# A two-layer vision tower: the late pieces of layer 1's feed-forward on earlier half-steps

## The chip, the cores and the metric

The kernel runs on one core of a Trainium2 chip. The metric is the device time of one execution in microseconds; before the change the median of three runs is 2030.3 us (2027.38 to 2031.56). All data are 32-bit floats.

## The reference

32 images of 256x256 pixels are cut into 256 tokens of width 256, and go through two layers of attention and feed-forward. The change touches the last part alone, the feed-forward of layer 1, a mixture of attention experts in four heads of width 64. Cut to what matters (n is the head, e the expert, d the width of a head):

```python
sx = einsum('bsh,ndh->bnsd', x, hl_w) + hl_b                  # head layer
q, k, v = ...                                                 # four experts' queries per head, one key, one value
att = softmax(einsum('bnesd,bntd->bnest', q, k) * d ** 0.5 + causal)
out = einsum('bnest,bntd->bnesd', att, v)
gs = softmax(einsum('bnsf,nef->bnse', out, gate_w) + gate_b)
mixed = einsum('bnsed,bnse->bnsd', out, gs)                   # experts mixed by their gates
hn = layernorm(mixed + resid)
hx = relu(fx @ fc1_w.T + fc1_b)                               # fx is hn; first layer
hx = layernorm(hx @ fc2_w.T + fc2_b + fx)                     # second layer, late norm
fg = softmax(fout @ fgate_w.T)                                # fout is hx, over the four heads
return fout * fg[..., None]                                   # added to h by the caller
```

## The kernel before

The stage works on an image in pieces, and each piece has a half-step at which it runs, counted from the image's own start. Images start six half-steps apart, so several are in flight, and the pieces of different images are interleaved. The order of instructions is fixed by the program: each engine works through its own instructions in the order in which this loop writes them, and an instruction that isn't ready holds up all that follow it on that engine.

```python
SCORES, VALUES, LAST = 6, 11, 46
EARLY = ((32, post, 9), (22, post, 15))
PIECES = (
    (0, prep, 0), (42, post, 12), (30, post, 16), (18, post, 1),
    (25, post, 5), (7, prep, 7), (31, post, 8), (19, post, 2),
    (26, post, 6), (44, post, 13), (2, prep, 2),
    (45, post, 14), (33, post, 10), (21, post, 3),
    (28, post, 7), (40, post, 11),
    (23, post, 4), (17, post, 0), (-1, prep, -1),
)

def pieces(t, table):
    for step, do, i in table:
        b, r = divmod(t - step, 6)
        if r == 0 and 0 <= b < B:
            do(b, images[b], i)

for t in range(-1, 6 * (B - 1) + LAST):
    active = [(images[b], t - 6 * b) for b in range(B)]
    if t % 2 == 0:
        ...                                  # scores of two parts, expert products (A), head values
        pieces(t, EARLY)
        ...                                  # masks and exponentials of the scores, copies of the products
    pieces(t, PIECES)
    ...                                      # values: exponentials times head values, at half-steps 11, 13, 15
```

An even half-step and the odd one after it make a round; the six half-steps from one image's start to the next are rounds one, two and three. In each round TensorE has scores (products of 64 rows, two at a time in the two halves of the rows), in rounds one and three expert products in the same form, and values (products of 64 columns, two at a time). A "full product" takes all 128 rows and all 128 columns.

The masks and exponentials (`weights`), with L1038 and L1040 of the profile:

```python
nc.vector.tensor_tensor(own, own, over(tri, [P, n_e, P], 1), ALU.add)     # L1038, in the scores' bank
t = pt.tile([P, 512], F32, name="et")
nc.scalar.activation(t, p, AF.Exp)                                        # L1040
```

The pieces that the change moves, and those on which they depend (cuts marked by dots):

```python
if i == 2:   ...                             # gates; both mixing products on GpSimd (L1118)
if i == 3:   ...                             # VectorE: sums of the mix, to im.r ("er")
if i == 15:  im.sq = squares(im.r)           # ScalarE
if i in (4, 10):
    nc.vector.tensor_reduce(ss, im.sq, AX.X, ALU.add)                     # L1131
    im.rs = head_rstd(ss)                                                 # GpSimd, L1069 and L1070 ("hv")
    if i == 10 and b % 8 == 7:
        check_ranges(b)                                                   # two VectorE instructions
if i == 5:
    nc.vector.tensor_tensor(im.r, im.r, over(im.rs, G8, 2), ALU.mult)     # L1136, er
if i == 6:
    p = feature_major(im.r...)                                            # four transposes of er
    nc.scalar.activation(im.fT..., p, AF.Identity, bias=col("e_b"), scale=col("e_g"))   # fxT
if i == 7:
    mm(p, fc1, im.fT...)                                                  # the first layer, a full product
    nc.scalar.activation(im.hx..., p, AF.Relu, bias=col("fc1_b"))
    ...                                                                   # four DMAs: both <- fxT, hx
if i == 8:   ...                             # second layer (W,both), VectorE copies to ey
if i == 9:   im.sq = squares(im.y[:, :, 0:HD])
if i == 11:  ...                             # VectorE: enorm <- ey * rs; head gate, its exponential
if i == 12:  ...                             # four transposes of enorm; ScalarE to foT
if i == 13:  ...                             # four transposes of foT (L1192)
if i == 14:  ...                             # VectorE: fout <- transposed * gate, + h; DMA to the output
```

All of TensorE's results go through eight PSUM banks of 512 columns, handed out in turn. `fxT`, `hx`, `both`, `enorm`, `foT` and `fout` have one buffer each, `ey` has two.

Of the kernel before, what the change touches and what calls it, by code (L numbers as in the profile page):

```python
# [79 lines left out]
def vit_tower(tc, a, out):  # L80
# [847 lines left out]
    with (  # L928
# [166 lines left out]
        def post(b, im, i):  # L1095
# [113 lines left out]


        images = [Image() for _ in range(B)]
        SCORES, VALUES, LAST = 6, 11, 46
        EARLY = ((32, post, 9), (22, post, 15))
        PIECES = (
            (0, prep, 0), (42, post, 12), (30, post, 16), (18, post, 1),
            (25, post, 5), (7, prep, 7), (31, post, 8), (19, post, 2),
            (26, post, 6), (44, post, 13), (2, prep, 2),
            (45, post, 14), (33, post, 10), (21, post, 3),
            (28, post, 7), (40, post, 11),
            (23, post, 4), (17, post, 0), (-1, prep, -1),  # L1220
        )

# [424 lines left out]
```

## Time and profile before

| What | us | share of the span |
| --- | --- | --- |
| span of the profiled run | 2025.9 | |
| TensorE busy | 1953.6 | 96% |
| VectorE busy | 1316.5 | 65% |
| ScalarE busy | 823.9 | 41% |
| GpSimd busy | 726.8 | 36% |
| layer 1's feed-forward, from the first mask to the end | 707.2 | 35% |
| of it, after the last mask | 67.8 | 3% |

In the profile PE is TensorE, PEld its loading of weights, DVE VectorE, ACT ScalarE and POOL GpSimd. A line of the order of time has the start of a group of like instructions, its length in us, the engine, the line of the program, the operation, what it writes and reads, and in brackets how long the engine sat idle before it and which instruction ended that. All matrix products have the line of one helper, L115, and are told apart by their tiles. The ends of matrix products are modelled, so starts are the safer times. Each product of 32-bit floats leaves two records.

### The profile page before, as it was taken

The numbers are of one execution on the slowest core, as the hardware profiler recorded it, in microseconds if no ns is written. First come the engines' busy times: TensorE is split into PE (matmuls) and PEld (weight loads), VectorE is DVE, ScalarE is ACT, GpSimd is POOL, SyncE is SP. The second block draws the span as 40 slices with busy tenths as digits, with TensorE's granted clock in tenths as the row PEclk, the third lists the DMA queues.
The fourth block names the chain that finished last, engine by engine and source line by source line (L and its number), as shares of the span: only waits on it lengthen the run. The fifth ranks groups of instructions, "written<-read, shape, count | busy, mean of one in ns | idle before, by whom it ended". The sixth has DMA issues, their size and how long they took to land.

```text
span 2025.9 us, 37649 instructions
## 1 busy us (share of the span) xinstructions
PE 1953.6 (96%) x15108; PEld 1374.2 (68%) x15108; DVE 1316.5 (65%) x3605; ACT 823.9 (41%) x1549; POOL 726.8 (36%) x692
## 2 busy tenths in 40 slices
PE   9998999999999989999899999999999999999984
PEld 8885676766666757666455555577777777777762
DVE  2335557676665653443556465567889999998986
ACT  0001312122222112212444444377777777777761
POOL 1224215243432342434333433203444443434443
PEclk9999999999999999999899999999999999999996
DMA  9440000000000141221000000001212121221211
GB/s 301 150 139 1 0 0 32 16 27 11 22 13 19 36 147 50 78 68 58 11 0 1 1 1 0 0 23 33 54 49 59 49 59 49 54 54 46 62 49 54
DMA packets 69813, 95.09 MB, mean 47 GB/s; under 512 B 8576, under 2 KB 51200, under 8 KB 69248
## 3 DMA queue, kind: packets, MB, share of 16 engines
q1 hardware_dynamic: 62912, 75.04, 13.0%
q0 software_dynamic: 6144, 16.79, 2.7%
q8 instruction: 121, 1.98, 0.4%
q10 hardware_dynamic: 576, 0.79, 0.1%
q14 instruction: 60, 0.49, 0.1%
HBM read 46.45 MB, written 20.97 MB: 33 GB/s over the span
## 4 chain that ended last, share of the span: by engine, by line
PE 94%; DVE 3%; ACT 1%; DMA 1%; POOL 0%; issue 0%; SPq 0%; ACTq 0%; DVEq 0%
PE bank L115 88%; PE bank L688 2%; PE bank L188 1%; PE bank L1192 1%; PE bank L350 0%; DMA both<-hx 0%; ACT bxT L193 0%; PE bank L241 0%; DVE fout L1201 0%; DMA tokW<-in_tokW_dram 0%; DVE bx L174 0%; DVE ctmp L357 0%; DVE fout L1197 0%; DVE two L1123 0%; DVE ctmp L355 0%
## 5 line engine op out<-in xcount | busy, mean ns | idle before, releaser
L1040 ACT ACTIVATE et<-bank 128x512 f32<-128x512 f32 x384 | 202.3, 598 | 58.5 <-DVE bank L1038 57.9
L115 PEld LDWEIGHTS bank<-ev,et 128*64 128x64 f32 x6144 | 198.4, 137 | 33.3 <-ACT et L1040 20.6
L115 PE MATMUL bank<-ev,et 128*64 128x74 f32 (+1 forms) x6144 | 211.3, 227 | 0.0
L1038 DVE TENSOR_TENSOR bank<-bank,w_tri 128x256 f32<-128x256 f32 (+1 forms) x384 | 173.6, 515 | 55.6 <-PE bank L115 53.7
L1118 POOL TENSOR_TENSOR eo<-eo,gate 128x1024 f32<-128x1024 f32 x64 | 121.9, 1925 | 215.7 <-DVE gate L1115 203.1
L115 PE MATMUL bank<-g,sx 64*128 64x512 f32 (+1 forms) x512 | 191.0, 502 | 1.4 <-ACT g L998 1.4
L115 PE MATMUL bank<-g,sw 64*128 64x512 f32 (+1 forms) x512 | 189.6, 502 | 0.0
L115 PE MATMUL bank<-tokW,patch 128*128 128x256 f32 x768 | 168.0, 382 | 0.3 <-DMA tokW<-in_tokW_dram 0.3
L115 PEld LDWEIGHTS bank<-tokW,patch 128*128 128x128 f32 x768 | 146.8, 191 | 21.6 <-DMA tokW<-in_tokW_dram 1.3
L115 PE MATMUL bank<-bxT,w_wuv 128*128 128x512 f32 x320 | 147.9, 601 | 6.6 <-ACT bxT L193 4.0
L193 ACT COPY bxT<-bank 128x512 f32<-128x512 f32 x16 | 9.4, 586 | 341.4 <-PE bank L188 341.4
L1070 POOL TENSOR_TENSOR hv<-hv,minus_half 128x8 f32<-128x8 f32 x64 | 119.6, 1868 | 5.3
L1056 ACT COPY eo<-bank 128x286 f32<-128x286 f32 x256 | 97.3, 421 | 58.5 <-PE bank L115 52.0
L115 PE MATMUL bank<-wvo,dm 128*128 128x512 f32 x256 | 114.0, 598 | 0.0
L115 PE MATMUL bank<-xsel,w_w 128*128 128x512 f32 x256 | 113.4, 601 | 0.0
L115 PE MATMUL bank<-attn,bv 128*128 128x256 f32 x512 | 113.3, 379 | 0.0
L115 PE MATMUL bank<-w_wo,gT 128*128 128x256 f32 x512 | 113.1, 379 | 0.0
L115 PE MATMUL bank<-w_w,hT 128*128 128x256 f32 x512 | 113.1, 379 | 0.0
L115 PE MATMUL bank<-w_wuv,bxT 128*128 128x512 f32 x256 | 112.5, 592 | 0.0
L115 PEld LDWEIGHTS bank<-attn,bv 128*128 128x128 f32 x512 | 97.1, 190 | 19.5 <-issue 6.7
L115 PEld LDWEIGHTS bank<-w_w,hT 128*128 128x128 f32 x512 | 96.7, 190 | 15.8 <-issue 3.4
L1069 POOL TENSOR_SCALAR hv<-ranges 128x8 f32<-128x8 f32 x64 | 39.1, 610 | 189.8 <-DVE ranges L1131 189.6
(258 smaller groups left out, 3861.8 us busy)
## 6 DMA issues: line engine op xcount, KB each, us to landing
patch<-in_patches_dram SPq DMA_DIRECT2D x31, 768.0 KB, 4.8
sw<-sx SPq DMA_DIRECT2D x64, 128.0 KB, 2.4
both<-fxT SPq DMA_DIRECT2D x64, 128.0 KB, 2.4
both<-hx SPq DMA_DIRECT2D x64, 128.0 KB, 2.3
out_dram<-fout SPq DMA_DIRECT2D x32, 256.0 KB, 2.4
cs<-ranked SPq DMA_DIRECT2D x32, 128.0 KB, 3.8
results<-cy SPq DMA_DIRECT2D x32, 128.0 KB, 1.7
w_w<-in_w_dram SPq DMA_DIRECT2D x2, 1024.0 KB, 6.1
```

What stands on the lines that cost most here:

```text
L115: nc.tensor.matmul(o, lhsT, rhs, start=first, stop=last)
L188: nc.tensor.transpose(p[:, o : o + P], x[:, c, k * P : (k + 1) * P], ident)
L193: nc.scalar.copy(o, i)
L688: nc.tensor.transpose(p[:, o : o + P], x[:, c, k * P : (k + 1) * P], ident)
L1038: nc.vector.tensor_tensor(own, own, over(tri, [P, n_e, P], 1), ALU.add)
L1040: nc.scalar.activation(t, p, AF.Exp)
L1056: nc.scalar.copy(im.o[:, c * NH + n, 0:OC], p[:, 0:OC])
L1069: nc.gpsimd.tensor_scalar(v, x, 1.0 / HD, 1e-8, ALU.mult, ALU.add)
L1070: nc.gpsimd.tensor_tensor(v, v, minus_half, ALU.pow)
L1118: nc.gpsimd.tensor_tensor(im.mix[k], im.mix[k], over(im.gate[:, :, 2 * k : 2 * k + 2], [P, NC * NH, 2, HD], 3), ALU.mult)
L1192: nc.tensor.transpose(im.po[:, o : o + P], im.fT[:, k, c * P : (c + 1) * P], ident)
```

## The change

Two things move, and nothing is added or removed. The last four pieces of an image (11 to 14: late norm, its transposes, the transposes back, the output) run six half-steps sooner, in the same places of a round, so that the loop is six half-steps shorter. The transposes of `er` (piece 6) move from the start of the second round to the end of the first, just behind the piece that makes `er`; and the first layer (piece 7) moves from the third round to the second. What it is for: with fc1 gone, the third round holds no full product among its products of half rows and half columns, and the schedule has a shorter tail.

```diff
-        SCORES, VALUES, LAST = 6, 11, 46
+        SCORES, VALUES, LAST = 6, 11, 40
         EARLY = ((32, post, 9), (22, post, 15))
         PIECES = (
-            (0, prep, 0), (42, post, 12), (30, post, 16), (18, post, 1),
-            (25, post, 5), (7, prep, 7), (31, post, 8), (19, post, 2),
-            (26, post, 6), (44, post, 13), (2, prep, 2),
-            (45, post, 14), (33, post, 10), (21, post, 3),
-            (28, post, 7), (40, post, 11),
+            (0, prep, 0), (36, post, 12), (30, post, 16), (18, post, 1),
+            (25, post, 5), (25, post, 6), (7, prep, 7), (31, post, 8), (19, post, 2),
+            (38, post, 13), (2, prep, 2), (26, post, 7),
+            (39, post, 14), (33, post, 10), (21, post, 3),
+            (34, post, 11),
             (23, post, 4), (17, post, 0), (-1, prep, -1),
         )
```

Within a round the order of VectorE's instructions stays as it was. TensorE's order changes: round one ends with the transposes of `enorm`, then those of `er`, then the second layer and the values; round two has scores, transposes of `foT`, head layer, first layer, values; round three has scores, expert products, values.

## The prediction

> **What bounds the kernel now.** I read the busy shares first, then the busy time by stage, then the order of time of single engines in one image of layer 1's feed-forward. Everything before that stage is untouched: the change moves pieces of this schedule alone.
>
> ```profile
> PE 1953.6 (96%) x15108; PEld 1374.2 (68%) x15108; DVE 1316.5 (65%) x3605; ACT 823.9 (41%) x1549; POOL 726.8 (36%) x692
> ```
>
> TensorE is busy almost throughout; but a share of the whole says nothing of one stage. The busy times of two stretches, 32 images in full swing and the run-out (columns: span, then busy us of each engine):
>
> ```profile
> 1431.63:1904.90 473.27, 473.27 (x7240) 369.03 (x7240) 429.25 (x1181) 358.87 (x783) 202.00 (x138) 1.00 0.21 53
> 1958.00:2025.90 67.90, 31.29 (x338) 23.23 (x332) 47.99 (x131) 18.54 (x39) 24.28 (x18) 0.69 0.19 52
> ```
>
> In full swing TensorE is busy 473.27 of 473.27 us, and the list of waits has no TensorE wait in that stretch; VectorE is busy 429.25, or 91%. So VectorE has little air. The run-out, 68 us, is a chain of latencies with TensorE less than half busy. Now one image, by TensorE's order of time (start, duration, in us):
>
> ```profile
> 1637.35 1.17 PE L115 MATMUL bank<-W,both 128*64 128x68 f32 x32
> 1638.35 2.16 PE L115 MATMUL bank<-ev,et 128*64 128x74 f32 x64
> ...
> 1642.36 0.66 PE L688 MATMUL bank<-ident,er 128*128 128x128 f32 x4
> 1642.86 0.60 PE L1192 MATMUL bank<-ident,foT 128*128 128x128 f32 x4
> 1643.29 1.89 PE L115 MATMUL bank<-exT,w_hl 128*128 128x256 f32 x8
> 1645.12 2.21 PE L115 MATMUL bank<-ev,et 128*64 128x74 f32 x64
> ...
> 1650.04 1.12 PE L115 MATMUL bank<-fxT,w_fc 128*128 128x512 f32 x2
> 1651.09 2.21 PE L115 MATMUL bank<-ev,et 128*64 128x74 f32 x64
> ...
> 1657.36 0.60 PE L688 MATMUL bank<-ident,enorm 128*128 128x128 f32 x4
> 1657.89 1.17 PE L115 MATMUL bank<-W,both 128*64 128x68 f32 x32
> ```
>
> The second layer (W,both) recurs after 1657.89 - 1637.35 = 20.54 us: the period of an image. The same image on VectorE:
>
> ```profile
> 1636.54 0.68 DVE L1136 TENSOR_TENSOR er<-er,hv 128x512 f32<-128x512 f32 x1
> ...
> 1641.60 1.96 DVE L1038 TENSOR_TENSOR bank<-bank,w_tri 128x512 f32<-128x512 f32 x4 [1.46 <-PE bank L115]
> ...
> 1648.73 1.95 DVE L1038 TENSOR_TENSOR bank<-bank,w_tri 128x256 f32<-128x256 f32 x4
> ...
> 1654.39 1.62 DVE L1038 TENSOR_TENSOR bank<-bank,w_tri 128x256 f32<-128x256 f32 x4
> ...
> 1657.08 0.69 DVE L1136 TENSOR_TENSOR er<-er,hv 128x512 f32<-128x512 f32 x1
> ```
>
> VectorE waits for TensorE once, 1.46 us before the second round's masks (L1038), and is then dense until L1136 has scaled `er`. That ends at 1637.22; TensorE passes from `enorm` to W,both at 1637.35. Only 0.13 us lie between them, and exactly there the change puts the transposes that read `er`. This is the line to watch.
>
> **What the Trainium skill says.** TensorEngine Tiling (Array Packing), Key Properties: changing the tiling mode drains TensorE. The trace agrees: the four expert products (sx,A, row halves) take 1655.92 - 1655.05 = 0.87 us before another product in row halves, but 0.96 before the full fc1; and fc1 takes 1.05 from its start to the next, where half of the 1.71 of w_hl (1.83 less some 0.12 for its own change of mode) is 0.86. SBUF — State Buffer, on the two separate sides: VectorE and GpSimd share a port pair, and the later of them blocks. The trace agrees: L1083 takes 0.26 at 1643.86 and ends with the gate products on GpSimd (1640.29 + 3.81 = 1644.10). Perfetto Trace Analysis, Tensor Engine Instruction: matmul ends are estimated. So I count from start to start.
>
> **The change part by part**, for one image. A round is two half-steps; rounds one, two and three make six.
>
> TensorE alone. The third round loses fc1: 0.96 + 1.05 = 2.01 become 0.87 plus one direct change from row to column halves, which no run shows yet; estimate 0.10, so 0.97. The second round gains fc1 behind other full products: 0.86. The four `er` transposes (0.5) move from round two to the end of round one, beside other transposes: nothing. Sum: 20.54 - 2.01 + 0.97 + 0.86 = 20.36, a gain of 0.18. No instruction disappears.
>
> The new wait. The `er` transposes now stand straight after L1136 and ahead of W,both. Follow the loop from the end of L1136 at 0. VectorE to TensorE takes 0.06 (in the run-out `enorm` ends at 2014.58 + 0.69 and its transposes start at 2015.33). Transposes to W,both 0.53 (1657.36 to 1657.89), W,both 1.00, values 2.09: the second round's scores start at 3.68, where they start at 1640.44 - 1637.22 = 3.22 now. Scores 1.92, foT 0.43, then w_hl and fc1 1.71 + 0.86 + 0.12 = 2.69, values 2.13: the third round's scores start at 10.85, against 1647.25 - 1637.22 = 10.03 now.
>
> The third of that round's four masks needs the last score. The first round shows how long that takes: its masks end at 1656.01, the last two take 0.33 + 0.42, so the third starts at 1655.26, 2.03 after the scores began at 1653.23 (and the 1.62 there, where four such masks take 4 x 0.33 + 0.1, shows the wait). In the third round the mask now starts at 1648.73 + 0.66 = 1649.39, or 12.17, and the last score would allow 12.06: 0.11 of slack. After the change it can't start before 10.85 + 2.03 = 12.88, 0.71 later. From there to the end of L1136 VectorE is dense. Without its small wait in round one that loop lasts 20.29 (L1136 at 1595.68 and 1615.97, while VectorE caught up), so 20.29 + 0.71 = **21.00 us per image**, 0.46 over 20.54. TensorE, able to do 20.36, would wait about 0.64 for `er` in every image.
>
> The sum over the stage. L1136 of the images ends at 1372.9 (image 0), 1925.2 (27), 1945.3 (28). The first periods, with little late work, gain less: +0.2 and +0.9, then +1.3 as the four late pieces join an image earlier. The 24 periods from image 3 to 27 last 1925.19 - 1431.63 = 493.6 now and 24 x 21.00 = 504.0 then: +10.4. Image 27 to 28: +0.2. In every eighth image the range check adds two instructions of some 0.6 us to VectorE. Today they are absorbed by its air (the periods then run 21.5 and 20.3, 20.3, ... with TensorE unmoved); in the new loop about 0.85 of 1.2 remains, three times: +2.5. Together +15.5.
>
> The run-out. Six half-steps less do not mean an image's work less: all pieces remain, and only the chain of image 31 counts. Its gain: `enorm` of image 31 now waits at 2014.58 behind the output of image 30, although its factor left GpSimd at 2010.75; fewer foreign pieces lie ahead of its end. I work this out as -2. Its loss: W,both now waits behind transposes that wait for `er`; near 1979 that shifts the second layer from 1978.3 to about 1980, near 1964 by some 1.4, and the late norm, now one half-step behind its GpSimd factor (about 2.6 us), waits 0.9 more. Together about +4; net +2. The total is 15.5 + 2 = +17.5, or 2048; because rival A pulls one way only, I put 2046.
>
> **Rivals.** A: TensorE stays the bound and keeps its 0.18 in all images, and the run-out shrinks by 2 to 6: 2030.3 - 5.8 - 4 = 2020. For it speaks that TensorE has no wait today and that 0.13 us are a positive slack; against it, that `er` itself hangs on TensorE's scores, so that the slack is consumed as soon as the transposes push them back. B: the new wait comes, but only the second round's masks hold VectorE back (4.84 against 4.38, of which L1083 hides 0.09): 20.29 + 0.37 = 20.66 per image, with the range checks at full length 24 x 0.12 + 3.6, and with the start and run-out about +9: 2039. C: the shorter tail is worth a whole image of the run-out, 10 to 15 us, and pays for everything: about 2030. Against it, that the last images are bound by VectorE, GpSimd and DMA in turn, whose work is all still there.
>
> **Range and chances.** The loop's sum has seven terms, each good to some 0.03; 0.2 per image either way are 5 us, the run-out is good to 6, and A or B might hold in part. So 2046 with 2033 to 2058. Two per cent are 40.6 us: slower by that much would need 1.4 us per image, faster has no mechanism. Faster 0.01, same 0.96, slower 0.03.
>
> **What would show it.** Right: a list of waits in full swing in which TensorE's transposes wait for VectorE's L1136, 0.3 to 0.7 us in each image; a period near 21.0; a small wait of L1038 for TensorE in round three, and about 1.8 in place of 1.46 in round two; experts straight into values within 1.0 us. Wrong: a period under 20.5 without that wait (A), one of 20.65 without a wait in round three (B), or a stage that ends more than 5 us earlier after image 31's `er` (C). The prediction would be wrong above all if VectorE's chain shortens where GpSimd's port no longer blocks it, or if the change of mode costs far more than 0.1.

## The result and the profile after

The change makes the kernel slower: 2054.4 us (median of four runs, 2053.7 to 2055.4) against 2029.9; the ratio is 1.0122, with a 95% interval of 1.0105 to 1.0140. The prediction said 2046 and 2033 to 2058.

First the busy times by stage, in the columns of the prediction (span, then busy us of PE, PEld, DVE, ACT and POOL): full swing from image 3's to image 27's L1136, then the run-out from the last mask.

```profile
1436.56:1948.17 511.61, 493.11 (x7536) 386.42 (x7536) 446.20 (x1231) 384.03 (x817) 210.93 (x144) 1.00 0.21 51
1982.00:2053.10 71.10, 27.78 (x322) 21.39 (x318) 45.15 (x120) 17.55 (x36) 23.91 (x18) 0.65 0.16 42
```

The same 24 images take 511.6 us where they took 493.6, and TensorE, which was busy for all of 493.6 us there, now idles for 18.5 us of 511.6. The list of waits for TensorE in full swing (1432 to 1925 us), which was empty before, has two rows (waiting engine and line, what released it, us in total, times, longest):

```profile
PE bank L688 <- DVE er L1136: 16.5, 23, 0.8
PE bank L115 <- ACT g L998: 1.3, 3, 0.4
```

There are 23 waits of 0.7 us, one in each image, for the instruction that scales `er`; the three of the second row fall in the three periods with a range check. Where the wait for `er` sits in TensorE's order of time, for one image:

```profile
1648.38 0.60 PE L688 MATMUL bank<-ident,enorm 128*128 128x128 f32 x4
1649.68 0.63 PE L688 MATMUL bank<-ident,er 128*128 128x128 f32 x4 [0.70 <-DVE er L1136]
1650.24 1.17 PE L115 MATMUL bank<-W,both 128*64 128x68 f32 x32
...
1655.25 0.66 PE L1192 MATMUL bank<-ident,foT 128*128 128x128 f32 x4
1655.74 1.89 PE L115 MATMUL bank<-exT,w_hl 128*128 128x256 f32 x8
1657.47 1.02 PE L115 MATMUL bank<-fxT,w_fc 128*128 128x512 f32 x2
1658.42 2.21 PE L115 MATMUL bank<-ev,et 128*64 128x74 f32 x64
...
1660.56 0.69 PE L115 MATMUL bank<-g,sw 64*128 64x512 f32 x1
...
1662.39 1.03 PE L115 MATMUL bank<-sx,A 64*128 64x256 f32 x8
1663.35 2.21 PE L115 MATMUL bank<-ev,et 128*64 128x74 f32 x64
...
1670.91 0.63 PE L688 MATMUL bank<-ident,er 128*128 128x128 f32 x4 [0.70 <-DVE er L1136]
```

What the change was for is there too: fc1 costs 0.95 beside other full products (1657.47 to 1658.42) where it cost 1.05, and the expert products go straight into values after 0.96 (1662.39 to 1663.35). But from one image's transposes of `er` to the next it is 21.23 us (1649.68 to 1670.91). VectorE in the same image:

```profile
1648.85 0.68 DVE L1136 TENSOR_TENSOR er<-er,hv 128x512 f32<-128x512 f32 x1
...
1654.49 1.96 DVE L1038 TENSOR_TENSOR bank<-bank,w_tri 128x512 f32<-128x512 f32 x4 [1.81 <-PE bank L115]
...
1661.72 0.76 DVE L1038 TENSOR_TENSOR bank<-bank,w_tri 128x256 f32<-128x256 f32 x2
1662.65 1.30 DVE L1038 TENSOR_TENSOR bank<-bank,w_tri 128x512 f32<-128x512 f32 x2 [0.17 <-PE bank L115]
...
1670.08 0.68 DVE L1136 TENSOR_TENSOR er<-er,hv 128x512 f32<-128x512 f32 x1
```

The wait in round two has grown from 1.46 to 1.81, and in round three, where the four masks were one dense group, the group is now split by a wait of 0.17 for the last score. VectorE waits for TensorE's scores, and TensorE waits for VectorE's `er`, once around in each image: neither is full, and the loop is the bound.

### The profile page after: what moved, and what is told of

It is laid out like the page before. It is cut to its first block, busy times and chain, and to the rows that moved or that the text cites. A ratio compares the mean times of both kernels' runs of the same rounds, so it can differ in the third digit from the quotient of the medians.

```text
span 2053.1 us, 37650 instructions
## 1 busy us (share of the span) xinstructions
PE 1952.3 (95%) x15108; PEld 1376.4 (67%) x15108; DVE 1313.7 (64%) x3605; ACT 834.9 (41%) x1549; POOL 726.1 (35%) x692
## 4 chain that ended last, share of the span: by engine, by line
PE 81%; DVE 15%; issue 1%; POOL 1%; ACT 1%; DMA 0%; SPq 0%; DVEq 0%; ACTq 0%
PE bank L115 77%; DVE bank L1038 4%; PE bank L688 1%; DVE ranges L1131 1%; PE bank L188 1%; DVE enorm L1172 1%; DVE er L1136 1%; DVE junk L982 1%; PE bank L1192 1%; DVE ex L174 1%; DVE sm_m L1075 1%; PE bank L350 0%; POOL hv L1070 0%; DVE lg L1104 0%; ACT bxT L193 0%
## 5 line engine op out<-in xcount | busy, mean ns | idle before, releaser
L1040 ACT ACTIVATE et<-bank 128x512 f32<-128x512 f32 x384 | 207.3, 599 | 75.8 <-DVE bank L1038 73.3
```

## The experiments

Theory: the loss is the loop `er` (VectorE) - its transposes, second layer, values, scores (TensorE) - masks (VectorE) - `er`. Rivals: the late pieces, now just behind their GpSimd factor, hold VectorE up; or the new order of TensorE's products (and with it the turns of the PSUM banks) costs in itself. Seven kernels, each compared with the kernel before on the same chip. The period is that of an undisturbed image; "24 images" is from image 3's L1136 to image 27's; "run-out" from image 28's L1136 to the end; all three are from the profiled run.

| kernel | median us | ratio to before (95%) | period | 24 images | run-out |
| --- | --- | --- | --- | --- | --- |
| before | 2028 to 2030 | | 20.53 | 493.6 | 80.6 |
| the change | 2054.4 | 1.0122 (1.0105 to 1.0140) | 21.23 | 511.6 | 84.3 |
| late pieces only | 2027.1 | 0.9991 (0.9984 to 0.9998) | 20.53 | 493.3 | 77.3 |
| `er` transposes and first layer only | 2054.0 | 1.0120 (1.0103 to 1.0137) | 21.23 | 511.7 | 86.3 |
| first layer back in round three | 2043.7 | 1.0065 (1.0048 to 1.0082) | 20.75 | 501.7 | 85.0 |
| `er` scaled earlier | 2030.3 | 1.0008 (0.9999 to 1.0017) | 20.34 | 491.1 | 85.3 |
| `er` transposes in round two | 2022.4 | 0.9974 (0.9967 to 0.9980) | 20.34 | 491.1 | 75.7 |
| `er` transposes behind W,both | 2031.0 | 1.0012 (1.0005 to 1.0019) | 20.64 | 497.4 | 76.6 |
| as the last but one, first layer in round three | 2027.3 | 0.9986 (0.9977 to 0.9994) | 20.53 | 493.3 | 77.7 |

**The late pieces only.** The kernel before, with

```diff
-        SCORES, VALUES, LAST = 6, 11, 46
+        SCORES, VALUES, LAST = 6, 11, 40
-  (42, post, 12)  (44, post, 13)  (45, post, 14)  (40, post, 11)
+  (36, post, 12)  (38, post, 13)  (39, post, 14)  (34, post, 11)
```

> Only the four late pieces run six half-steps sooner; the transposes of er and the first layer stay where they were. Theory (the loss is the new loop er - transposes - scores - masks - er, and the late pieces have no part in it): the period of an image stays 20.5 us, the run-out gets 2 to 4 us shorter, about 2027. Rival (the late pieces, now one half-step behind their GpSimd factor, hold VectorE up and cost the period): period near 21.2 and about 2050.

Measured: 2027.1, period 20.53, run-out 3.2 shorter. The late pieces cost no period: that rival falls.

**The transposes of er and the first layer only.** The change, with the late pieces back on 40, 42, 44, 45 and LAST 46.

> Only the transposes of er and the first layer move; the late pieces stay on their old half-steps. Theory (new loop): period 21.2 us as in the whole change, TensorE waits about 0.7 us for L1136 in each image, and without the gain of the late pieces in the run-out about 2057. Rival (late pieces): period near 20.4, about 2026.

Measured: 2054.0, period 21.23. The whole loss is in this half. I had expected 3 us more: beside this half the late pieces gain only 2.0 in the run-out (86.3 to 84.3), and they cost 1.2 in the first images (image 0's L1136 to image 3's lasts 60.15 here and 61.31 in the change).

**The first layer back in round three.**

```diff
-            (38, post, 13), (2, prep, 2), (26, post, 7),
+            (38, post, 13), (2, prep, 2),
-            (34, post, 11),
+            (28, post, 7), (34, post, 11),
```

> As the whole change, but the first layer goes back to the third round; only the er transposes stay behind L1136. Theory (two gates in series: the second round's masks, and, because fc1 stands ahead of it, the third round's masks): the wait of L1038 in the third round disappears, the second round's remains near 1.8 us, and the period falls from 21.23 to about 20.8; about 2043. If the transposes alone made the whole loss, the period stays at 21.2 and the time at 2054; if fc1's place made it, the period is 20.5 and the time about 2032.

Measured: 2043.7, period 20.75. VectorE's order of time for one image of this kernel:

```profile
1664.46 0.68 DVE L1136 TENSOR_TENSOR er<-er,hv 128x512 f32<-128x512 f32 x1
1670.10 1.96 DVE L1038 TENSOR_TENSOR bank<-bank,w_tri 128x512 f32<-128x512 f32 x4 [1.81 <-PE bank L115]
1677.12 1.95 DVE L1038 TENSOR_TENSOR bank<-bank,w_tri 128x256 f32<-128x256 f32 x4
1682.73 1.41 DVE L1038 TENSOR_TENSOR bank<-bank,w_tri 128x256 f32<-128x256 f32 x4
1685.21 0.68 DVE L1136 TENSOR_TENSOR er<-er,hv 128x512 f32<-128x512 f32 x1
```

Round two's wait stays at 1.81, and round three's masks are dense again (1.95 in one group). TensorE still waits for `er`, but so briefly that no bracket marks it; the starts show it:

```profile
1685.41 0.60 PE L688 MATMUL bank<-ident,enorm 128*128 128x128 f32 x4
1686.04 0.63 PE L688 MATMUL bank<-ident,er 128*128 128x128 f32 x4
```

From `enorm` to `er` it is 0.63, where the next kernel, with `er` there in time, has 0.44; and 1686.04 is 0.15 after the end of L1136 (1685.21 + 0.68 = 1685.89). So the 0.70 us of the period are two gates in series: 0.22 from the transposes of `er` (20.75 - 20.53), and 0.48 from fc1 standing ahead of round three's scores (21.23 - 20.75).

**er scaled earlier on VectorE.**

```diff
-            (0, prep, 0), (36, post, 12), (30, post, 16), (18, post, 1),
-            (25, post, 5), (25, post, 6), (7, prep, 7), (31, post, 8), (19, post, 2),
+            (0, prep, 0), (36, post, 12), (24, post, 5), (30, post, 16), (18, post, 1),
+            (25, post, 6), (7, prep, 7), (31, post, 8), (19, post, 2),
```

> As the whole change, but VectorE scales er (L1136) ahead of the zero count and of the gate's row in the same round, some 1.15 us sooner; no TensorE instruction moves. Theory (TensorE waits for L1136): the loop becomes 21.23 - 1.15 = 20.1 us, TensorE is the bound again at 21.23 - 0.84 = 20.4, the wait for L1136 is gone except after range checks; about 2032 (the run-out stays some 4 us longer than before). Rival (the order of TensorE's products, changes of mode and weight loads make the loss): the period stays at 21.2 and the time at 2054.

Measured: 2030.3, period 20.34, with the order of TensorE's instructions, and the turns of the banks with it, as in the change. TensorE's order of time has the three groups without a gap:

```profile
1676.42 0.60 PE L688 MATMUL bank<-ident,enorm 128*128 128x128 f32 x4
1676.86 0.60 PE L688 MATMUL bank<-ident,er 128*128 128x128 f32 x4
1677.39 1.17 PE L115 MATMUL bank<-W,both 128*64 128x68 f32 x32
```

The second rival falls: the order of products is no loss, but a gain of 0.19 once `er` is there in time. Yet the total does not beat the kernel before: the run-out, counted from an L1136 that stands earlier in its round here, is still 85 us.

**The transposes of er behind the second layer.**

```diff
-  (25, post, 5), (25, post, 6), (7, prep, 7), (31, post, 8), (19, post, 2),
+  (25, post, 5), (7, prep, 7), (31, post, 8), (25, post, 6), (19, post, 2),
```

> As the whole change, but within the first round the transposes of er stand behind the second layer (W,both) in place of ahead of it. Theory: the second layer's 1.00 us falls out of the loop, 21.23 - 1.00 = 20.2, so TensorE is the bound at 20.34 and up to 0.2 for two more changes of mode, 20.5; in the run-out the second layer no longer waits for er, so that the last image's chain gets back the 4 to 5 us which the change and the early er both lost there; about 2027. If the run-out's loss has another cause (the late norm half a round behind its factor), the run-out stays at some 84 us after image 28's er and the time is about 2034.

Measured: 2031.0, period 20.64, run-out 76.6. Right on the run-out, too low by 4 us on the time: four transposes between products of column halves cost 0.30 an image more than beside other transposes, where I allowed 0.2 (the period is 20.64, and 20.34 with `er` scaled earlier; TensorE has no wait for `er` in either). In the run-out TensorE's order of time of the change has, for images 30 and 31,

```profile
2005.74 1.09 PE L688 MATMUL bank<-ident,er 128*128 128x128 f32 x4 [3.22 <-DVE er L1136]
2006.76 2.08 PE L115 MATMUL bank<-W,both 128*64 128x68 f32 x32
...
2023.69 1.09 PE L688 MATMUL bank<-ident,er 128*128 128x128 f32 x4 [3.18 <-DVE er L1136]
2024.71 2.06 PE L115 MATMUL bank<-W,both 128*64 128x68 f32 x32
```

and with the transposes behind:

```profile
1980.10 2.08 PE L115 MATMUL bank<-W,both 128*64 128x68 f32 x32
1983.40 1.08 PE L688 MATMUL bank<-ident,er 128*128 128x128 f32 x4 [1.22 <-DVE er L1136]
1995.06 2.08 PE L115 MATMUL bank<-W,both 128*64 128x68 f32 x32
1998.31 1.09 PE L688 MATMUL bank<-ident,er 128*128 128x128 f32 x4 [1.17 <-DVE er L1136]
```

Above, the second layer, whose input was sent on its way some 11 us earlier (the DMA from `hx` is issued at 1995.87), waits behind transposes that wait 3.2 us, and the images come 17.95 us apart (2005.74 to 2023.69); below, it runs first and they come 14.91 apart. With this order alone the run-out's whole loss is gone (76.6, against 84.3 in the change and 80.6 before).

**The transposes of er in round two, first layer behind them.** The transposes go back behind round two's scores, but `fxT` is taken ahead of that round's exponentials on ScalarE, so that fc1 finds it ready at the end of the same round. The late pieces are early, as in the change.

```diff
-        EARLY = ((32, post, 9), (22, post, 15))
+        EARLY = ((32, post, 9), (26, post, 6), (22, post, 15))
-  (25, post, 5), (25, post, 6), (7, prep, 7),
+  (25, post, 5), (7, prep, 7),
```

> As the whole change, but the transposes of er stay in the second round, straight behind its scores, with fxT taken ahead of that round's exponentials on ScalarE, so that the first layer can still follow at the end of the same round. Theory (the loss is the loop through L1136; the third round without a full product is worth 0.2 us an image in itself): no wait of TensorE for L1136, period near 20.4 where the range checks don't disturb it, the run-out 3 us or more shorter as with the late pieces alone; about 2022. If moving the first layer is of no worth, it equals the late pieces alone, 2027; if fc1 ahead of the third round's scores is the harm, the period is over 20.8.

Measured: 2022.4, 0.26% under the kernel before (0.20 to 0.33). The list of TensorE's waits in full swing (1432 to 1925) has none for L1136, only three, in the periods with a range check:

```profile
PE bank L115 <- ACT g L998: 2.2, 3, 0.7
```

It beats both kernels.

**The same, with the first layer left in round three.** `(26, post, 7)` goes back to `(28, post, 7)` ahead of `(34, post, 11)`.

> As the version with the er transposes in the second round and fxT ahead of the exponentials, but the first layer stays in the third round. If the 0.19 us an image of that version come from the full product leaving the third round, the period is 20.53 again and the time that of the late pieces alone, 2027; if they come from the new place of fxT on ScalarE, the period stays at 20.34 and the time at 2022.

Measured: 2027.3, period 20.53, run-out 77.7. So the 0.19 us an image comes from the first layer's move out of round three to the full products of round two, not from the new place of `fxT`; the move gains 2.0 in the run-out as well (77.7 to 75.7). The same move costs 0.48 an image where the transposes of `er` stand straight behind L1136 (20.75 to 21.23).

## Why the prediction was right, and where it was off

The mechanism was right step by step: the wait of TensorE for L1136 (0.64 foretold, 0.70 measured), about 1.8 us in place of 1.46 in round two, a small wait in round three (0.17), experts into values within 1.0 (0.96), TensorE able to do 20.36 (20.34 where `er` is early). Rivals A and B fall with the waits shown above: A with the wait for L1136, B with the wait in round three. C falls with the end of the stage: from image 31's L1136 to the end it is 29.5 us, against 31.9 before, so the shorter tail is worth 2.4 us and not 10 to 15. B's sum does describe another kernel: with fc1 back in round three the second round's gate alone remains, at 20.75 where B said 20.66.

The loss was put at 16 us and is 24.5. Within layer 1's feed-forward, from its first mask, the profiled runs differ by 24.8 us (707.2 and 732.0):

- **The period, the term that was mis-sized most.** 21.00 foretold, 21.23 measured. VectorE to TensorE takes 0.15 and not 0.06 (L1136 ends at 1649.53, the transposes start at 1649.68). I had taken one pair of the run-out, the shortest there; others show more, as 1999.13 + 0.68 = 1999.81 to 1999.96. Then transposes to W,both 0.56 for 0.53, the first transposes after the scores 0.49 for 0.43 (1655.25 to 1655.74), and the third mask 2.09 after the scores for 2.03 (1660.56 to 1662.65). Together 0.24. The third of these could have been read in the prediction's own lines: the 0.43 was that of the second group of transposes, and the group that stood straight behind the scores took 0.50 (1642.36 to 1642.86). Over 24 images full swing costs +18.0, with the range checks, against 10.4 + 2.5.
- **The range checks.** Such a period is 21.93, 0.70 over the others, for 0.85 foretold, and nothing is recovered after it. Right.
- **The first images and image 27 to 28.** +2.6 and +0.4, for +2.4 and +0.2. Right in sum; the first three periods themselves changed by -0.2, +1.2 and +1.6, for +0.2, +0.9 and +1.3.
- **The run-out.** +3.8, for +2. The gain at the end is 2.4, for 2; the delay of images 28 to 31 is 6.1, for 4. The cause that I gave first, the second layer behind transposes that wait, is shown by moving it: 76.6 in place of 84.3. The wait of the late norm for its GpSimd factor (0.80 at 2000.59 and again at 2018.59) comes on top. From image 28's L1136 to image 31's it is 48.7 us before, 53.0 with the transposes and the first layer moved alone, and 54.8 in the change: the last two periods are 17.11 and 17.05 without the early late pieces, 18.01 and 17.95 with them. So the early late pieces add 0.9 in each of these two, about as much as the late norm waits there, where the sum had 0.9 once; the rest is 4.3, where the sum had 3.1.
- **The last step, 2046 for a sum of 2047.8 "because rival A pulls one way only", was a mistake in kind:** the loop had been worked out, and a rival that denies the loop can't take a part of it back. The four of its terms that were off were all too short.

## What to carry to other kernels

In a fixed schedule on in-order engines, measure the time from the end of an instruction to the place where a reader would wait for it before moving the reader there; then follow the loop on to the same instruction one period later, since a slack of 0.13 us that hangs on the waiting engine itself is used up at once. A piece that must wait should not stand ahead of one that is ready. Here the good half of the change could be had by moving less: the first layer one round earlier, with its transposes left in place (2022.4).

## What the runs showed that I had not expected

Two engines that are each less than full can bind each other: with TensorE busy 96% and VectorE 87% of full swing (493.11 and 446.20 of 511.61), neither share shows the loss of 0.7 us an image, only the waits do. Four 128x128 transposes cost 0.30 us more between column-half products than beside other full ones (20.64 against 20.34), 0.15 on average for each of the two changes between column halves and full products that this adds. The change from row halves straight to column halves cost 0.09 (the expert products take 0.96 before values, 0.87 before more products in row halves), no more than the change to a full product, before which they took 0.96 as well.
